# Transposing the norms' results on VectorE and by DMA instead of on TensorE, in a graph network and attention kernel

## The chip, the cores and the metric

The kernel runs on one core of a Trainium2 chip. The metric is the device time of that core in microseconds, from its first to its last instruction. Most executions of a kernel agree within 0.3%. A kernel under test and the kernel before it ran in turn on the same chip.

Engines in the profile: PE is TensorE (matrix products, and transposes as products with a unit matrix), DVE is VectorE, ACT is ScalarE, POOL is GpSimd, SP is the engine that issues most DMAs. PEclk is the share of the full clock that TensorE was granted.

## The reference, cut to what matters

```python
x   = graph_layer(x, adj, ...)     # 64 graphs, 256 nodes, 256 features, fp32
out = relational_attention(x, adj, ...)

def graph_layer(x, adj):
    h = gat(gat(x, adj, W1, a), adj, W2, a)
    h = layernorm(x + h) * g1 + b1                       # norm 0
    return layernorm(h + relu(h @ wf1 + bf1) @ wf2 + bf2) * g2 + b2    # norm 1

def relational_attention(x, adj):
    q, k, v_r = x @ Wq + bq, x @ Wk + bk, x @ Wv[r] + bv[r]
    p = softmax(q k^T / sqrt(32))                        # 8 heads
    a = sum over r of (p * (adj == r)) @ v_r
    x = layernorm(x + a @ Wo + bo) * g3 + b3             # norm 2
    return layernorm(x + gelu(x @ W1 + b1) @ W2 + b2) * g4 + b4        # norm 3
```

Only relations 0 and 1 occur, so the kernel keeps `v0` and `v1 - v0`. In these data all norm scales are 1 and all shifts and biases 0; the kernels do not rely on it unless it is said.

## The kernel before

Two graphs make a unit of 512 nodes, and 32 units go through a software pipeline. A turn handles attention and its feed-forward part of unit y, the first feed-forward part of unit y+1 and the graph attention of unit y+2. A norm's result lies with nodes on partitions; the product that follows needs features on partitions. So there are three transposed features in a turn: h1T (after norm 0, for the first feed-forward part), h2T (after norm 1, for q, k and v) and h3T (after norm 2, for the second feed-forward part).

```python
def to_features(src, name, scale=None, shift=None):
    dst = work.tile([P, KB, TN], F32, tag="hT", name=name)
    for k in range(KB):                                   # 2
        ps = bank(f"{name}p{k}")                          # one of 6 PSUM banks
        for t in range(T):                                # 4
            nc.tensor.transpose(ps[:, t * P:(t + 1) * P], src[:, t, k * P:(k + 1) * P], ident)
        ...                                               # VectorE: out of PSUM, * scale + shift

def normed(u, l, y, ...):
    ...                                                   # VectorE: bn_stats, mean, variance
    nc.vector.tensor_scalar(ve, variance, EPS, ...)       # 128x4
    nc.gpsimd.tensor_tensor(rs, ve, mhalf, ALU.pow)       # 128x4
    for t in blocks:                                      # VectorE: (y - mean) * rs, in place
        nc.vector.tensor_scalar(y[:, t, :], y[:, t, :], mv[:, t, 0:1], rs[:, t:t + 1], ...)

def affine(u, l, xn, g, b, r=None):                       # the norm's scale and shift: the residual
    ...                                                   # r: 128 x (4*256)
    nc.gpsimd.tensor_mul(r, xn, g[:, None, :].to_broadcast(list(r.shape)))
    nc.gpsimd.tensor_add(r, r, b[:, None, :].to_broadcast(list(r.shape)))

def weighted(u, b, m, q, k_, aT):                         # "scores": one graph, four heads
    ...                                                   # PE: 8 products into 4 banks (sp)
    for a in range(HPB):                                  # ScalarE: e = exp(sp)
        nc.scalar.activation(e[:, a, :], ps[a], AF.Exp, scale=isd)
    for a in range(0, HPB, 2):                            # VectorE: ea = e * mask, 128x1024 twice
        nc.vector.tensor_tensor(ea[:, a:a + 2, :], e[:, a:a + 2, :],
                                ab[:, None, :].to_broadcast([P, 2, NB * N]), ALU.mult)
    nc.vector.tensor_add(es, e[:, :, 0:N], e[:, :, N:2 * N])
```

The order of TensorE in a turn: h2T, the second graph sums (ygp), q, k, two blocks of v, h1T, two blocks of v, scores 0, hidden 0 to 2, scores 1, sums 0 (po, zo), and so on. Each block of v takes a PSUM bank until VectorE has added the bias and written it to SBUF. Only TensorE's order is fixed by hand; the other engines' orders come from a scheduler.

Of the kernel before, what the change touches and what calls it, by code (L numbers as in the profile page):

```python
# [16 lines left out]
P = 128  # L17
# [368 lines left out]
def narrow_path(  # L386
# [42 lines left out]
    def load(u):  # L429


        xs = io.tile([P, T, F], F32, tag="xs", name=f"xs{u}")
        nc.sync.dma_start(xs, x[G * u:G * (u + 1)].rearrange("b (c p) f -> p (b c) f", p=P))
        xq = io.tile([P, KB, TN], F32, tag="xq", name=f"xq{u}", bufs=1)
        aq = io.tile([P, T, N], I32, tag="aq", name=f"aq{u}", bufs=1)
        xu = x[G * u:G * (u + 1)].rearrange("b (n r) (k q c) -> q k r (b n) c", r=32, k=KB, c=32)
        au = adj[G * u:G * (u + 1)].rearrange("b (n r) (j q c) -> q b r j n c", r=32, j=NB, c=32)
        for q in range(Q):
            qp = slice(q * 32, (q + 1) * 32)
            for k in range(KB):  # L440
                nc.sync.dma_start(xq[qp, k, :].rearrange("r (n c) -> r n c", c=32), xu[q, k])
            for b in range(G):
                nc.sync.dma_start(aq[qp, b * NB:(b + 1) * NB, :].rearrange("r j (n c) -> r j n c", c=32),
                                  au[q, b])
        return xs, xq, aq
# [50 lines left out]
    def row(v, name):  # L496
        n = v.shape[0]
        t = const.tile([P, n], F32, name=name)
        nc.sync.dma_start(t, bass.AP(tensor=v.tensor, offset=v.offset, ap=[[0, P], [1, n]]))
        return t  # L500
# [42 lines left out]
    rbf2, rbo, rbt2 = row(g_bf2, "rbf2"), row(t_bo, "rbo"), row(t_b2, "rbt2")  # L543
# [13 lines left out]
    nc.gpsimd.tensor_add(rb1, rb1, rbf2)  # L557
    nc.gpsimd.tensor_add(rb2, rb2, rbo)
    nc.gpsimd.tensor_add(rb3, rb3, rbt2)


    def to_features(src, name, scale=None, shift=None):

        dst = work.tile([P, KB, TN], F32, tag="hT", name=name)
        for k in range(KB):
            ps = bank(f"{name}p{k}")
            for t in range(T):
                nc.tensor.transpose(ps[:, t * P:(t + 1) * P], src[:, t, k * P:(k + 1) * P], ident)
            if scale is None:
                nc.vector.tensor_copy(dst[:, k, :], ps)  # L570
            else:
                nc.vector.tensor_scalar(dst[:, k, :], ps, scale[:, k:k + 1], shift[:, k:k + 1],  # L572
                                        op0=ALU.mult, op1=ALU.add)
        return dst

    def adjacency(u, aq):
# [3 lines left out]
        return aT  # L580

# [18 lines left out]
    def projected(u, hT):  # L600
        xp = work.tile([P, T, WX], F32, tag="wh", name=f"xp{u}")
        for t in range(T):
            ps = bank(f"xpp{u}_{t}")
            for k in range(KB):
                nc.tensor.matmul(ps[:, :WX], hT[:, k, t * P:(t + 1) * P], gwe[:, k, :],  # L605
# [82 lines left out]
    def hidden(u, l, hT, wi, bi, func, blocks, h1=None):  # L688
# [3 lines left out]
        for f in blocks:  # L692
            ps = bank(f"h1p{u}_{l}_{f}")
            for k in range(KB):
                nc.tensor.matmul(ps, wi[:, k, f * P:(f + 1) * P], hT[:, k, :],  # L695
# [3 lines left out]

    def hidden_out(u, l, h1, wo_, res):  # L700
        y = work.tile([P, T, F], F32, tag="y", name=f"yf{u}_{l}")
        for b in range(G):
            add_blocks(u, f"yfp{l}_", y, res, b, lambda t, k: h1[:, k, t * P:(t + 1) * P],
                       lambda b, k: wo_[:, k, :], FB)
        return y

    def queries_keys(u, hT):
        qk = []
        for w, c, name in ((wq, bq, "q"), (wk, bk, "k")):
            d = work.tile([P, KB, TN], F32, tag=name, name=f"{name}{u}", bufs=1)  # L710
            for m in range(KB):
                ps = bank(f"{name}p{u}_{m}")
                for k in range(KB):
                    nc.tensor.matmul(ps, w[:, k, m * P:(m + 1) * P], hT[:, k, :],  # L714
# [5 lines left out]
    def values(u, hT, blocks, v=None):  # L720
# [3 lines left out]
        for t in blocks:  # L724
            ps = bank(f"vp{u}_{t}")
            for k in range(KB):
                nc.tensor.matmul(ps, hT[:, k, t * P:(t + 1) * P], wvf[:, k, :],  # L727
# [53 lines left out]
    def early(z):  # L781

        d = g[z]
        d["xT"] = work.tile([P, KB, TN], F32, tag="hT", name=f"xT{z}")
        nc.vector.transpose(d["xT"].rearrange("p k n -> p (k n)"), d["xq"].rearrange("p k n -> p (k n)"))
# [14 lines left out]
    def second_sums(x_):  # L800
# [8 lines left out]
        d["res"] = affine(x_, 0, d["y"], rg1, rb1)  # L809
# [3 lines left out]
    def out_pieces(u, h1, res):  # L813
# [3 lines left out]
        for b in range(G):  # L817
            ps = bank(f"yfp1_{u}_{b}")
            for i in range(NB):
                t = b * NB + i  # L820
                for k in range(FB):
                    nc.tensor.matmul(ps[:, i * F:(i + 1) * F], h1[:, k, t * P:(t + 1) * P], w2[:, k, :],  # L822
                                     start=(k == 0), stop=(k == FB - 1))
                if i == NB - 1:
                    bt = slice(b * NB, (b + 1) * NB)
                    nc.vector.tensor_tensor(y[:, bt, :].rearrange("p t f -> p (t f)"), ps,
                                            res[:, bt, :].rearrange("p t f -> p (t f)"), ALU.add)
                    normed(u, 3, y, range(b * NB, (b + 1) * NB))
                    affine(u, 3, y[:, bt, :], rg4, rb4, r[:, bt, :])
                    nc.sync.dma_start(out[G * u + b].rearrange("(c p) f -> p c f", p=P), r[:, bt, :])  # L830
                yield

    def piece(_=None):
# [3 lines left out]
    def turn(y_, x_, z):  # L837
        def have(u):
            return 0 <= u < NG

        if y_ == 0:
            g[z]["xs"], g[z]["xq"], g[z]["aq"] = load(z)
        if z + 1 < NG:
            g[z + 1]["xs"], g[z + 1]["xq"], g[z + 1]["aq"] = load(z + 1)
        Y, X, Z = g.get(y_, {}), g.get(x_, {}), g.get(z, {})
        if have(y_):
            hT = to_features(Y["y"], f"h2T{y_}", lg2, lb2)
        if have(x_) and y_ > 0:
            second_sums(x_)
        if have(y_):  # L850
            q, k_ = queries_keys(y_, hT)
            v = values(y_, hT, range(T // 2))
        if have(x_):
            h1hT = to_features(X["y"], f"h1T{x_}", lg1, lb1)
        if have(y_):
            values(y_, hT, range(T // 2, T), v)
            quads = [(b, m) for b in range(G) for m in range(KB)]
            aT = Y["aT"]
            oT = q
            acc = [None] * G  # L860
            e = {}

            def scores(n):
                e[n] = weighted(y_, *quads[n], q, k_, aT)

            def apply_(n):
                b, m = quads[n]
                if m == 0:
                    acc[b] = [psum.tile([P, 512], F32, tag=t_, name=f"{t_}{y_}_{b}") for t_ in ("po", "zo")]
                applied(b, m, v, *e.pop(n), *acc[b])  # L870
                if m == KB - 1:
                    divided(y_, b, *acc[b], oT)

        h1 = None

        def steps():
            if have(y_):
                yield scores, 0
            yield hid, range(0, 3)
            if have(y_):  # L880
                yield scores, 1
                yield piece, None
                yield apply_, 0
            yield hid, range(3, 4)
            if have(y_):
                yield scores, 2
                yield apply_, 1
            yield hid, range(4, 6)
            if have(y_):
                yield scores, 3  # L890
                yield piece, None
            yield hid, range(6, 8)
            if have(z):
                yield early, z
            if have(y_):
                yield apply_, 2
                yield apply_, 3

        def hid(blocks):
            nonlocal h1  # L900
            if have(x_):
                h1 = hidden(x_, 0, h1hT, wf1, bf1, AF.Relu, blocks, h1)

        for do, what in steps():
            do(what)
        if have(y_):
            yo = work.tile([P, T, F], F32, tag="y", name=f"yo{y_}")

            def out_(b):
                add_blocks(y_, "yop", yo, Y["res"], b, lambda t, k: oT[:, k, t * P:(t + 1) * P],  # L910
                           lambda b, k: wo[:, k, :], KB)
            out_(0)
            piece()
        if have(z):
            project(z)
        if have(y_):
            out_(1)
        if have(z):
            first_scores(z)
        if have(y_):  # L920
            yn = normed(y_, 2, yo)
            res = affine(y_, 2, yn, rg3, rb3)
            piece()
        if have(x_):
            yf = hidden_out(x_, 0, h1, wf2, X["res"])
            X["y"] = normed(x_, 1, yf)
            X["res"] = affine(x_, 1, X["y"], rg2, rb2)
        if have(y_):
            hT = to_features(yn, f"h3T{y_}", lg3, lb3)
        if have(z):  # L930
            Z["hp"] = gat_first(z, Z["s"], Z["xp"])
        if have(y_):
            h1 = hidden(y_, 1, hT, w1, b1, AF.Gelu, range(FB))
        if have(z):
            second_scores(z)
            checked(z, Z["aq"])
        if y_ == NG - 2:
            left.append(out_pieces(y_, h1, res))
        elif y_ == NG - 1:
            for _ in out_pieces(y_, h1, res):  # L940
                pass
        else:
            yf = hidden_out(y_, 1, h1, w2, res)
            yn = normed(y_, 3, yf)
            res = affine(y_, 3, yn, rg4, rb4)
            nc.sync.dma_start(out[G * y_:G * (y_ + 1)].rearrange("b (c p) f -> p (b c) f", p=P), res)
# [78 lines left out]
```

## Time and profile before

| | before |
|---|---|
| time, median of 6 runs | 3293.18 us (3292.28 to 3294.46) |
| TensorE busy | 3244.5 us, 99% of 3290.2 |
| VectorE, ScalarE, GpSimd busy | 56%, 32%, 29% |
| a turn | 100.6 us |
| the 24 transposes of a turn | 2.63 us |

The prediction shows how these are read. Two timelines of the kernel before, GpSimd's and VectorE's (start, duration, engine, line, operation, output and inputs with their shapes, count; in brackets the idle time before it and what ended it):

```profile
2017.82 2.37 POOL L684 TENSOR_TENSOR res<-yg,rg 128x1024 f32<-128x1024 f32 x1 [1.50 <-DVE yg L676]
2020.27 2.36 POOL L685 TENSOR_TENSOR res<-res,rb 128x1024 f32<-128x1024 f32 x1
```

```profile
2025.48 2.36 DVE L751 TENSOR_TENSOR ea<-e,aT 128x1024 f32<-128x1024 f32 x2 [0.33 <-ACT e L749]
```

The last residual ends at 2022.63, the first masking starts at 2025.48. Its two instructions take 2.36 us together, 1.18 us each.

### The profile page before, as it was taken

The numbers are of one execution on the slowest core, as the hardware profiler recorded it, in microseconds if no ns is written. First come the engines' busy times: TensorE is split into PE (matmuls) and PEld (weight loads), VectorE is DVE, ScalarE is ACT, GpSimd is POOL, SyncE is SP. The second block draws the span as 40 slices with busy tenths as digits, with TensorE's granted clock in tenths as the row PEclk, the third lists the DMA queues.
The fourth block names the chain that finished last, engine by engine and source line by source line (L and its number), as shares of the span: only waits on it lengthen the run. The fifth ranks groups of instructions, "written<-read, shape, count | busy, mean of one in ns | idle before, by whom it ended". The sixth has DMA issues, their size and how long they took to land.

```text
span 3290.2 us, 42867 instructions
## 1 busy us (share of the span) xinstructions
PE 3244.5 (99%) x17468; PEld 2105.4 (64%) x17468; DVE 1853.9 (56%) x3611; ACT 1050.6 (32%) x1860; POOL 960.7 (29%) x822
## 2 busy tenths in 40 slices
PE   7999999999999999999999999999999999999997
PEld 5656666666666566666666665666666666656655
DVE  3654556655556545566555565455665555654545
ACT  3233233332332332333323323323333233233221
POOL 2223323233232233232332322332323323223322
PEclk9999999999999999999999999999999999999999
DMA  5110001101011100011010111000110101110000
GB/s 140 20 25 21 20 14 27 26 20 24 9 26 27 25 22 20 14 26 27 20 24 10 26 27 25 21 20 14 27 27 20 24 10 26 26 24 10 7 1 14
DMA packets 294859, 76.65 MB, mean 23 GB/s; under 512 B 254936, under 2 KB 294016, under 8 KB 294656
## 3 DMA queue, kind: packets, MB, share of 16 engines
q1 hardware_dynamic: 293248, 72.52, 10.0%
q8 instruction: 139, 2.28, 0.3%
q0 software_dynamic: 1056, 1.05, 0.2%
q14 instruction: 64, 0.52, 0.1%
q10 hardware_dynamic: 352, 0.28, 0.0%
HBM read 57.04 MB, written 16.78 MB: 22 GB/s over the span
## 4 chain that ended last, share of the span: by engine, by line
PE 96%; DVE 1%; issue 1%; DMA 1%; POOL 0%; SPq 0%; ACT 0%; ACTq 0%; POOLq 0%; DVEq 0%
PE h1p L695 27%; PE yfp L654 26%; PE po L764 7%; PE vp L727 7%; PE sp L743 4%; PE yop L654 3%; PE qp L714 3%; PE hpp L643 3%; PE xpp L605 3%; PE kp L714 3%; PE ygp L654 3%; PE zo L767 2%; PE rows L615 1%; PE yfp L822 1%; DVE rz L772 0%
## 5 line engine op out<-in xcount | busy, mean ns | idle before, releaser
L697 ACT ACTIVATE h<-h1p,cols 128x512 f32<-128x512 f32 x512 | 353.0, 690 | 531.2 <-PE h1p L695 530.0
L695 PE MATMUL h1p<-h1T,wf 128*128 128x512 f32 x1024 | 474.3, 606 | 0.1
L654 PE MATMUL yfp<-wf,h 128*128 128x256 f32 x2048 | 447.3, 379 | 0.0
L695 PE MATMUL h1p<-h3T,w 128*128 128x512 f32 x1024 | 445.4, 593 | 1.8 <-DVE h3T L572 1.8
L654 PEld LDWEIGHTS yfp<-wf,h 128*128 128x128 f32 x2048 | 386.8, 190 | 51.8 <-issue 0.5
L654 PE MATMUL yfp<-w,h 128*128 128x256 f32 x1920 | 419.4, 379 | 0.0
L751 DVE TENSOR_TENSOR ea<-e,aT 128x1024 f32<-128x1024 f32 x256 | 320.2, 1291 | 162.9 <-ACT e L749 162.9
L654 PEld LDWEIGHTS yfp<-w,h 128*128 128x128 f32 x1920 | 362.5, 190 | 48.0
L773 POOL TENSOR_TENSOR low<-low,rz 128x512 f32<-128x512 f32 x64 | 82.4, 1288 | 1002.2 <-DVE rz L772 1002.2
L749 ACT ACTIVATE e<-sp 128x512 f32<-128x512 f32 x512 | 264.2, 604 | 301.3 <-PE sp L743 300.0
L695 PEld LDWEIGHTS h1p<-h3T,w 128*128 128x128 f32 x1024 | 194.2, 190 | 234.2 <-issue 228.6
L695 PEld LDWEIGHTS h1p<-h1T,wf 128*128 128x128 f32 x1024 | 184.8, 190 | 232.5 <-issue 178.0
L624 DVE SCALAR_TENSOR_TENSOR s<-s 128x512 f32<-128x512 f32 x128 | 87.1, 681 | 427.3 <-ACT s L621 426.1
L657 DVE TENSOR_TENSOR yf<-yfp,res 128x512 f32<-128x512 f32 x124 | 85.8, 692 | 395.4 <-PE yfp L654 393.4
L685 POOL TENSOR_TENSOR res<-res,rb 128x1024 f32<-128x1024 f32 (+1 forms) x130 | 301.1, 2316 | 10.2
L672 POOL TENSOR_TENSOR rs<-ve,mhalf 128x4 f32<-128x4 f32 (+1 forms) x130 | 131.0, 1008 | 414.1 <-DVE ve L671 413.9
L727 PE MATMUL vp<-wv,h2T 128*128 128x512 f32 x512 | 230.1, 592 | 0.0
L772 DVE RECIPROCAL rz<-zo 128x512 f32<-128x512 f32 x64 | 214.6, 3354 | 4.9 <-PE zo L767 2.5
L716 ACT ACTIVATE q<-qp,cols 128x512 f32<-128x512 f32 x64 | 44.0, 687 | 530.6 <-PE qp L714 530.6
L645 ACT COPY hp<-hpp 128x258 f32<-128x258 f32 x128 | 47.3, 375 | 423.6 <-PE hpp L643 423.6
L684 POOL TENSOR_TENSOR res<-yf,rg 128x1024 f32<-128x1024 f32 (+1 forms) x66 | 151.0, 2288 | 96.2 <-DVE yf L676 95.4
L727 PEld LDWEIGHTS vp<-wv,h2T 128*128 128x128 f32 x512 | 94.9, 190 | 107.6 <-issue 107.6
(408 smaller groups left out, 4210.4 us busy)
## 6 DMA issues: line engine op xcount, KB each, us to landing
xs<-in_x_dram SPq DMA_DIRECT2D x32, 512.0 KB, 3.7
xq<-in_x_dram SPq DMA_DIRECT2D x240, 64.0 KB, 2.2
aq<-in_adj_dram SPq DMA_DIRECT2D x240, 64.0 KB, 2.4
out_dram<-res SPq DMA_DIRECT2D x30, 512.0 KB
wf<-in_L_gnn_w_ff_dram SPq DMA_DIRECT2D x2, 1024.0 KB, 7.2
w<-in_L_gnn_W_dram SPq DMA_DIRECT2D x2, 1024.0 KB
first<-in_adj_dram POOLq DMA_DIRECT2D x2, 512.0 KB, 7.5
out_dram<-res SPq DMA_DIRECT2D x4, 256.0 KB, 2.1
```

Of the source, the lines that this page charges most:

```text
L654: nc.tensor.matmul(ps[:, i * F:(i + 1) * F], lhs(t, k), rhs(b, k), start=(k == 0), stop=(k == n - 1))
L684: nc.gpsimd.tensor_mul(r, xn, g[:, None, :].to_broadcast(list(r.shape)))
L685: nc.gpsimd.tensor_add(r, r, b[:, None, :].to_broadcast(list(r.shape)))
L695: nc.tensor.matmul(ps, wi[:, k, f * P:(f + 1) * P], hT[:, k, :], start=(k == 0), stop=(k == KB - 1))
L697: nc.scalar.activation(h1[:, f, :], ps, func, bias=bi[:, f:f + 1])
L714: nc.tensor.matmul(ps, w[:, k, m * P:(m + 1) * P], hT[:, k, :], start=(k == 0), stop=(k == KB - 1))
L727: nc.tensor.matmul(ps, hT[:, k, t * P:(t + 1) * P], wvf[:, k, :], start=(k == 0), stop=(k == KB - 1))
L743: nc.tensor.matmul(ps[a][:, j * N:(j + 1) * N], k_[hp, m, j0:j0 + P], q[hp, m, b * N:(b + 1) * N], start=True, stop=True)
L749: nc.scalar.activation(e[:, a, :], ps[a], AF.Exp, scale=isd)
L751: nc.vector.tensor_tensor(ea[:, a:a + 2, :], e[:, a:a + 2, :], ab[:, None, :].to_broadcast([P, 2, NB * N]), ALU.mult)
L764: nc.tensor.matmul(po[hp, m * N:(m + 1) * N], vs[:, hp], w[:, a, j * N:(j + 1) * N], start=(n == 0), stop=(n == len(terms) - 1))
L772: nc.vector.reciprocal(rz, zo)
```

## The change

The intent is to take the three transposes of a turn off TensorE, which bounds the kernel. VectorE transposes 32x32 blocks, each within its own 32 partitions, and 16 DMAs carry the blocks to their partitions. As no eviction is left that could apply a norm's scale and shift, these are folded into the next weights and biases at the start. To give the DMAs time, ygp moves to the end of the turn before, and the first scores go ahead of v. The order of SP is now fixed by hand too.

```diff
+    def normed_features(u, l, xn, natural=False):
+        yt = work.tile([P, Q, KB, T, 32], F32, tag="yt", name=f"yt{u}_{l}", bufs=1)
+        for t in range(T):
+            nc.vector.transpose(yt[:, :, :, t].rearrange("p q k r -> p k q r"),
+                                xn[:, t].rearrange("p (k q c) -> p k q c", k=KB, c=32))
+        ...                                  # h2T (natural): the same with runs of 128 bytes
+        hT = work.tile([P, Q, KB, T, 32], F32, tag="hT", name=f"hT{u}_{l}")
+        for q in range(Q):
+            for a in range(Q):
+                nc.sync.dma_start(hT[q * 32:(q + 1) * 32, a], yt[a * 32:(a + 1) * 32, q])
+        return [hT[:, :, k].rearrange("p a t r -> p t a r") for k in range(KB)]
...
+    shifted(wf1, FB, lb1, bf1, "bf1")        # bias += weights^T shift, on TensorE; also wq, wk, w1, wv
+    for w, scale in ((wf1, lg1), (wq, lg2), (wk, lg2), (wv..., lg2), (w1, lg3)):
+        for k in range(KB):
+            nc.gpsimd.tensor_scalar(w[:, k], w[:, k], scale[:, k:k + 1], 1.0, ...)
...
     def turn(y_, x_, z):
-        hT = to_features(Y["y"], f"h2T{y_}", lg2, lb2)
-        second_sums(x_)
         q, k_ = queries_keys(y_, hT)
-        v = values(y_, hT, range(T // 2))
-        h1hT = to_features(X["y"], f"h1T{x_}", lg1, lb1)
-        values(y_, hT, range(T // 2, T), v)
-        scores 0; hidden 0-2; scores 1; sums 0; hidden 3; scores 2; sums 1; hidden 4-5; scores 3; ...
+        scores(0)
+        v = values(y_, hT, range(T))
+        scores(1); sums(0); hidden 0-1; scores(2); sums(1); hidden 2-4; scores(3); hidden 5-7; ...
...
-        hT = to_features(yn, f"h3T{y_}", lg3, lb3)
+        hT = normed_features(y_, 2, yn)
...
+        for t in range(T):
+            if t == T - 1:
+                second_sums(z)               # ygp and norm 0, one turn earlier
+            hidden_out_block(y_, 1, yf, h1, w2, res, t)
+        first_residual(z)                    # GpSimd: affine of norm 0
+        yn = normed(y_, 3, yf)
+        res = affine(y_, 3, yn, rg4, rb4)    # GpSimd: affine of norm 3
```

(The lines of the turn are abridged.)

## The prediction

> **What bounds the kernel now.** 64 graphs go through in 32 units of two; a software-pipelined turn handles three units at once (attention and feed-forward of unit y, first feed-forward of y+1, graph attention of y+2). I read the page's busy row and its chain first, to see which engine sets the end.
>
> ```profile
> PE 3244.5 (99%) x17468; PEld 2105.4 (64%) x17468; DVE 1853.9 (56%) x3611; ACT 1050.6 (32%) x1860; POOL 960.7 (29%) x822
> ...
> PE 96%; DVE 1%; issue 1%; DMA 1%; POOL 0%; SPq 0%; ACT 0%; ACTq 0%; POOLq 0%; DVEq 0%
> ```
>
> TensorE is the path; nothing else reaches 60%. A removed matmul is therefore worth its full pitch, and an added wait of TensorE costs its full length. Then TensorE in order of time over one turn in the middle (start, duration, group; durations overlap in the pipeline, so I use differences of starts):
>
> ```profile
> 2023.20 1.15 PE L743 MATMUL sp<-q,k 32*128 32x256 f32 x16
> ...
> 2072.39 1.04 PE L568 MATMUL h3T19p<-ident,yo 128*128 128x128 f32 x8
> 2073.27 3.65 PE L643 MATMUL hpp<-xp,s 128*128 128x258 f32 x16
> ...
> 2104.74 1.04 PE L568 MATMUL h2T20p<-ident,yf 128*128 128x128 f32 x8
> 2105.61 3.62 PE L654 MATMUL ygp<-hp,s 128*128 128x256 f32 x16
> ...
> 2119.36 1.04 PE L568 MATMUL h1T21p<-ident,yg 128*128 128x128 f32 x8
> 2120.24 3.60 PE L727 MATMUL vp<-wv,h2T 128*128 128x512 f32 x8
> ...
> 2123.77 1.15 PE L743 MATMUL sp<-q,k 32*128 32x256 f32 x16
> ```
>
> No line carries a wait. A turn is 2123.77 - 2023.20 = 100.57 us, and 30 like it follow from 112.5. The three groups of eight transposes hold TensorE for 0.88, 0.87 and 0.88 us: 2.63 us a turn. That is all that the change can take out of a turn. Last the start, where TensorE does wait (brackets: idle before):
>
> ```profile
> 14.34 1.18 PE L590 MATMUL aTp<-ident,first 128*128 128x128 f32 x8
> ...
> 22.88 1.04 PE L568 MATMUL xT1p<-ident,xs 128*128 128x128 f32 x8
> 32.00 5.26 PE L605 MATMUL xpp<-gwe,xT 128*128 128x260 f32 x16 [8.08 <-DVE xT L570]
> ...
> 96.02 5.40 PE L714 MATMUL qp<-h2T,wq 128*128 128x512 f32 x8 [2.05 <-DVE h2T L572]
> ```
>
> **What the Trainium skill says.** "VectorE: DVE Perf Modes", section "The three transpose paths": VectorE transposes 32x32 blocks only, TensorE a whole 128x128 into PSUM. So the blocks must still be moved between partitions, here by 16 DMAs each. The trace has the form: the transpose of 128x1024 fp32 (xT) takes 1.24 us, which I read as some 0.3 to 0.4 us for 128x256. "DMA: Bandwidth & Descriptors", section "Anatomy of one DMA", puts the fixed cost of a DMA at about 2 us, mostly the receipt of the write. The trace agrees: 64 KB pieces land 2.2 us (xq) and 2.4 us (aq) after their issue. "TensorE: Matmul & The Clock Gate", section "What's actually happening": after an idle window of about 3.4 us the array runs at half clock until warm. The trace agrees: the 16 xpp instructions after 8.08 us idle took 5.26 us, in the middle of the run 3.67 us.
>
> **What is removed.** Of 96 transposed features (3 for each of 32 units) three stay on TensorE (h1T of unit 0, h2T of unit 0, h3T of unit 31). 93 x 0.877 = 81.6 us leave TensorE's path. VectorE loses 186 evictions with scale and shift of 0.79 us, some 140 us, and gets 93 x 4 = 372 transposes of 128x256, about as much. Off the path, so neutral.
>
> **What is added in a turn.** Per feature: four VectorE transposes (about 1.5 us), 16 DMAs of 32 KB from one queue, and the landing. The issue is the long part. In the before trace eight xq issues took 4.05 us and cost 0.31 to 0.49 us each; small two-dimensional ones cost 0.24 to 0.28:
>
> ```profile
> 2025.18 4.05 SPq L441 DMA_DIRECT2D xq<-in_x_dram  x8
> ```
>
> I take 0.33 us for h1T and h3T (32 runs of 1 KB) and 0.45 for h2T (runs of 128 B): 16 x 0.33 = 5.3 us or 7.2 us, plus 2 us. With 1.5 us in front the added latency is about 9 us, or 11. Does TensorE reach the consumer earlier? Counting with pitches of the trace (0.429 us for a 512-wide instruction, 0.216 for 256):
>
> h3T: the norm's last pass ends at 2065.6 here.
>
> ```profile
> 2063.80 1.83 DVE L676 TENSOR_SCALAR yo<-yo,mv,rs 128x256 f32<-128x256 f32 x4 [1.00 <-POOL rs L672]
> ```
>
> Transposed by 2067.1, issued by 2072.5, landed by 2074.5. It is wanted after yfp and hpp, 2076.75 - 0.88 = 2075.9. Slack 1.3 us: the tightest.
> h1T: made near the end of the turn before, about 3 us after q's start in the new order; landed at 10.5; wanted after q, k, scores, v, scores and the first sums, at 18.2. Slack near 8 us.
> h2T: yf is normed 5 us after its matmuls, lands some 18 us after them, wanted 35 us after them.
> The new order also leaves 8 us instead of 6.4 between a unit's first scores and their sums. VectorE has v's four evictions in there and is some 9 us in arrears from the two norms, but by my count is ready by 15.6 for 15.9. Buffers: hT has two, and in the new order each is read before it is refilled. So a turn should be 100.57 - 2.63 = 97.9 us, with a chance of a small wait at h3T.
>
> **What is added once, at the start.** The folding of shifts is 40 matmuls of one column (80 instructions) and two of 512. The order of instructions puts all of them on TensorE ahead of aTp, and the last 16 need w1, one of the last weights to come. Before, aTp began at 14.34. The queue moves 300 to 370 GB/s; the bytes up to w1 are 7.9 MB, passed at about 27 us, landed at 28 to 29. The 16 matmuls are 32 instructions at 0.11 us warm or 0.22 cold (gwap in the trace has 0.22), some 5 us; rbv's four take 1.7. So aTp begins near 35. From aTp to the second xpp it is VectorE and ScalarE, some 13.7 us by the durations of the trace (transposes 2, copies with the check 2.5, xpp 3.9, rows 0.9, the softmax's first passes with the second check 4.4); the old run had 17.7, 8 of it waiting, since VectorE stood behind wv:
>
> ```profile
> 27.27 0.69 DVE L551 TENSOR_TENSOR wv<-wv 128x512 f32<-128x512 f32 x1 [9.28 <-DMA wv<-in_L_gnn_Wv_dram]
> ```
>
> The new xpp comes at 48.7 instead of 32.0: about 17 us late (14 to 19). The scaling of weights on GpSimd (some 11 us) ends before its first softmax work.
> A second loss is before turn 0. VectorE's order has h2T0's copies behind the whole norm of unit 1 and its four transposes. Before they ran ahead of it:
>
> ```profile
> 95.18 0.79 DVE L572 TENSOR_SCALAR h2T<-h2T0p,cols 128x512 f32<-128x512 f32 x1
> ...
> 99.16 1.38 DVE L676 TENSOR_SCALAR yg<-yg,mv,rs 128x256 f32<-128x256 f32 x4 [1.13 <-POOL rs L672]
> ```
>
> The norm ends at 100.5 (it waits for GpSimd's residual), transposes 102.0, first copy 102.65: q starts 6.6 us later.
>
> **At the end.** In turn 30 q follows directly on 13.7 us of hidden matmuls; h2T of unit 31 needs about 15.5: a wait of 2 us for 0.56 before. Two waits for h3T (0.9) go, and v between the first scores of turn 31 should save 2 us of the waits there. Sum -1.5.
>
> **Sum.** 3293.4 - 81.6 + 17 + 6.6 - 1.5 = 3233.9. For a chance of about one third that h3T or a bank waits, 0 to 1 us in 30 turns, I add 2: 3236, 1.7% faster.
>
> **Rivals.** (1) The start costs little, because the weights come earlier or the loss is caught up: nothing on TensorE in the start waits for data after qp, so what is lost there stays lost; but with w1 at 26 and a warm clock the loss is 20 instead of 24, and 3230. With no loss at all it would be 3212, 2.5% faster. (2) The DMAs come too late for h3T every turn: if an issue takes 0.45 us instead of 0.33, 1.9 us more, so 0.6 us a turn, about 18 us, and 3252; at 0.6 us an issue it is 3 us a turn and the change is worth nothing (3325). For it: aq's issues with four dimensions do take 0.63; against: this transfer has two dimensions, and the 128-row loads with 1 KB rows take 0.43. (3) VectorE becomes the bound in the first third of a turn, where its arrears hold back a PSUM bank and so k or the scores: 0.8 us of slack at k's second bank; a slower strided transpose, or a wait for a port while GpSimd works, would make it 0.5 us a turn, 15 us, 3250. (4) Moving operands in 128-byte runs are read more slowly: no such case is in the trace; half of the 512-wide matmuls of hidden would be hit. I think it unlikely.
>
> **Range and chances.** The gain in the turns is nearly certain in size, 81 us; the losses range from 20 to 60. That gives 3216 to 3262. The 2% line is 3227.5, 8 us under my number, and only a smaller loss in the start gets there: 0.22. Slower by 2% needs over 4 us of waiting a turn: 0.03.
>
> **What would show it.** Right: a turn of 97.9 us with no wait of TensorE; aTp near 35; a wait of about 9 us before the first qp; hT issues near 0.33 us. Wrong: h1p waiting for hT's DMA in each turn, a turn over 98.5, aTp before 30, or hidden's instructions off their 0.429 us pitch.

## The result and the profile after

The changed kernel takes 3512.59 us (median of 6 runs, 3506.42 to 3528.74) against 3293.18 us. The ratio is 1.0672, with a 95% interval of 1.0651 to 1.0692. Ratios here are the mean time of one kernel's fast runs over that of the other's of the same rounds, so not quite the ratio of the medians. The prediction was 3236 us with a range up to 3262. It was wrong.

The page's busy row and its chain of waits, after:

```profile
PE 3345.5 (95%) x16808; PEld 2103.9 (60%) x16808; DVE 1991.0 (56%) x3802; ACT 1054.2 (30%) x1860; POOL 994.2 (28%) x832
...
PE 71%; DVE 15%; SPq 8%; DMA 2%; POOL 2%; issue 1%; ACT 1%; DVEq 0%; ACTq 0%; POOLq 0%
```

TensorE was 96% of the chain; now VectorE holds 15% of it and the issuing of DMAs 8%. TensorE is busy for 101.0 us more with 660 fewer instructions. 81.6 us of transposes are gone, so what is left takes 182.6 us longer. Most of this is slow clock: the mean granted clock was 0.961 over 3527.0 us, against 0.996 over 3290.2 us before, which makes about 138 us of lost clock against 13 (one minus the clock, times the span). The folding's instructions at the start are some 20 us of the rest, and waits too short to be listed are in it too. Idle time rose from 45.7 to 181.5 us, 135.8 more. The two together, less the 81.6, are the 236.8 us between the spans of the two profiles, 3527.0 and 3290.2. (The profiled execution is the longest of the six, 3528.7 us, 16 us above the median.)

The view of TensorE's waits (what waited, for what: total us, times, longest):

```profile
PE h1p L737 <- DMA hT<-yt: 78.8, 30, 3.5
PE sp L799 <- DVE v L785: 52.7, 30, 1.9
```

Two waits that come once in nearly every turn are new: hidden (h1p) waits for h3T's DMAs, and the second scores (sp) wait for VectorE to clear a bank of v. TensorE in order of time over a turn:

```profile
2022.82 13.97 PE L737 MATMUL h1p<-hT,w 128*128 128x512 f32 x32 [2.33 <-DMA hT<-yt]
...
2061.30 1.15 PE L799 MATMUL sp<-q,k 32*128 32x256 f32 x16
...
2071.88 1.72 PE L799 MATMUL sp<-q,k 32*128 32x256 f32 x12 [1.74 <-DVE v L785]
2073.53 1.86 PE L820 MATMUL po<-e,v 128*32 128x256 f32 x16
...
2129.19 16.05 PE L737 MATMUL h1p<-hT,w 128*128 128x512 f32 x30 [3.48 <-DMA hT<-yt]
```

The three lines of eight transposes are gone, as intended. The wait of 1.74 us is followed by slow instructions: the 16 po products take 1.86 us here and 1.07 us at the next sums. The hidden after 3.48 us takes over 16 us; after 2.33 us it takes its full-clock 13.97. The mean turn is 107.5 us where 97.9 was predicted.

**The first wait** starts at the queue. SP's timeline, the 16 copies of the h3T that made TensorE wait 3.48 us:

```profile
2116.70 10.90 SPq L621 DMA_DIRECT2D hT<-yt  x16
```

This is 0.68 us an issue, and the slowest of the 31 h3T: most take 10.0 us, 0.63 us an issue. A copy lands 1.9 us after its own issue begins (median). Over all turns, TensorE comes to hidden 9.1 us after h3T's last block transpose, and the copies are complete 11.7 us after it; the difference is the mean wait of 2.6 us.

**The second wait** starts on GpSimd. GpSimd's and VectorE's timelines in the same turn:

```profile
2055.96 2.35 POOL L726 TENSOR_TENSOR res<-yg,rg 128x1024 f32<-128x1024 f32 x1 [1.50 <-DVE yg L718]
2058.39 2.35 POOL L727 TENSOR_TENSOR res<-res,rb 128x1024 f32<-128x1024 f32 x1
...
2063.36 2.36 POOL L726 TENSOR_TENSOR res<-yf,rg 128x1024 f32<-128x1024 f32 x1 [1.50 <-DVE yf L718]
2065.80 3.21 POOL L727 TENSOR_TENSOR res<-res,rb 128x1024 f32<-128x1024 f32 x1
```

```profile
2058.82 1.94 DVE L713 TENSOR_SCALAR ve<-mv 128x4 f32<-128x4 f32 x1
...
2063.58 6.51 DVE L807 TENSOR_TENSOR ea<-e,aT 128x1024 f32<-128x1024 f32 x2 [0.29 <-ACT e L805]
...
2071.15 2.47 DVE L785 TENSOR_TENSOR v<-vp,rbv 128x512 f32<-128x512 f32 x4
```

The residuals of norms 0 and 3 now lie on top of norm 3's passes and the first masking. A 128x4 instruction takes 1.94 us (0.17 where GpSimd is idle) and ends when the GpSimd instruction does. The two ea take 6.51 us instead of 2.36. That is what comes out if the first runs when `res<-yf,rg` has ended, at 2065.72, and the second when `res<-res,rb` has ended, at 2069.01: with its 1.18 us the second would end at 2070.19, and the two do end at 2070.09. GpSimd's 3.21 us instead of 2.35 are the other side of it. V's evictions stand behind them on VectorE. That VectorE and GpSimd can exclude each other for whole instructions is what the Trainium skill says in "SBUF — State Buffer", section "SBUF: two separate sides": they share a pair of ports, held as an exclusive lock for the whole instruction, by a VectorE instruction in a two-port mode or with two SBUF inputs (the latter only against a GpSimd instruction that reads SBUF), or by GpSimd's. The trace agrees, to a tenth of a microsecond.

**The start** went as predicted within a few microseconds (aTp: transposes of the first adjacency; xpp: the graph layer's first products; the last line is the first q):

```profile
36.67 1.91 PE L632 MATMUL aTp<-ident,first 128*128 128x128 f32 x8
...
50.22 6.81 PE L647 MATMUL xpp<-gwe,xT 128*128 128x260 f32 x16 [2.95 <-DVE xT L594]
...
122.91 6.25 PE L770 MATMUL qp<-h2T,wq 128*128 128x512 f32 x8 [8.38 <-DVE h2T L594]
```

The first q starts 26.9 us later than before (96.02).

### The profile page after: what moved, and what is told of

Read it like the earlier page. It is cut to its first block, busy times and chain, and to the rows that moved or that the text cites. A ratio compares the mean times of both kernels' runs of the same rounds, so it can differ in the third digit from the quotient of the medians.

```text
span 3527.0 us, 43810 instructions
## 1 busy us (share of the span) xinstructions
PE 3345.5 (95%) x16808; PEld 2103.9 (60%) x16808; DVE 1991.0 (56%) x3802; ACT 1054.2 (30%) x1860; POOL 994.2 (28%) x832
## 4 chain that ended last, share of the span: by engine, by line
PE 71%; DVE 15%; SPq 8%; DMA 2%; POOL 2%; issue 1%; ACT 1%; DVEq 0%; ACTq 0%; POOLq 0%
PE h1p L737 27%; PE yfp L748 13%; PE po L820 8%; SPq L621 7%; DVE ea L807 6%; PE sp L799 5%; PE xpp L647 3%; PE yop L696 3%; PE qp L770 3%; PE kp L770 3%; PE ygp L696 3%; PE zo L823 2%; DMA hT<-yt 2%; DVE yo L718 1%; DVE s L669 1%
## 5 line engine op out<-in xcount | busy, mean ns | idle before, releaser
L807 DVE TENSOR_TENSOR ea<-e,aT 128x1024 f32<-128x1024 f32 x256 | 424.7, 1699 | 265.1 <-ACT e L805 264.0
L737 PE MATMUL h1p<-hT,w 128*128 128x512 f32 x992 | 476.7, 642 | 81.4 <-DMA hT<-yt 78.8
L748 PE MATMUL yfp<-w,h 128*128 128x256 f32 x2048 | 452.9, 379 | 0.0
L737 PE MATMUL h1p<-hT,wf 128*128 128x512 f32 x992 | 451.5, 603 | 0.0
L748 PEld LDWEIGHTS yfp<-wf,h 128*128 128x128 f32 x2048 | 387.9, 191 | 52.3 <-issue 0.5
L748 PEld LDWEIGHTS yfp<-w,h 128*128 128x128 f32 x2048 | 386.6, 190 | 52.3 <-issue 0.8
L737 PEld LDWEIGHTS h1p<-hT,w 128*128 128x128 f32 x992 | 202.0, 207 | 343.0 <-issue 337.6
L727 POOL TENSOR_TENSOR res<-res,rb 128x1024 f32<-128x1024 f32 (+1 forms) x130 | 326.8, 2514 | 10.2
L737 PEld LDWEIGHTS h1p<-hT,wf 128*128 128x128 f32 x992 | 181.8, 191 | 233.5 <-issue 186.4
L799 PE MATMUL sp<-q,k 32*128 32x256 f32 x2048 | 201.5, 426 | 52.7 <-DVE v L785 52.7
L799 PEld LDWEIGHTS sp<-q,k 32*128 32x128 f32 x2048 | 116.6, 192 | 175.3 <-issue 96.0
L783 PE MATMUL vp<-wv,hT 128*128 128x512 f32 x496 | 221.1, 599 | 0.0
```

The source lines that it names most:

```text
L737: nc.tensor.matmul(ps, wi[:, k, f * P:(f + 1) * P], hT[k], start=(k == 0), stop=(k == KB - 1))
L748: nc.tensor.matmul(ps[:, i * F:(i + 1) * F], h1[:, k, t * P:(t + 1) * P], wo_[:, k, :], start=(k == 0), stop=(k == FB - 1))
L783: nc.tensor.matmul(ps, hT[k][:, t * P:(t + 1) * P], wvf[:, k, :], start=(k == 0), stop=(k == KB - 1))
L799: nc.tensor.matmul(ps[a][:, j * N:(j + 1) * N], k_[hp, m, j0:j0 + P], q[hp, m, b * N:(b + 1) * N], start=True, stop=True)
```

## The experiments

The theory: the change loses (A) about 2.6 us a turn and some slow clock because one queue takes 10 to 11 us to issue 16 copies, and (B) about as much because GpSimd's residuals hold the masking up, and it behind v. The rival to B: VectorE is simply in arrears with its own new work, and the long ea is a side effect. Thirteen kernels were run, all with correct results. The times of the kernel before in their rounds lie between 3292.4 and 3294.0 us (medians).

| run | what it is | us | ratio to before |
|---|---|---|---|
| after | the change | 3512.6 | 1.067 |
| e1 | h3T back on TensorE | 3416.5 | 1.037 |
| e2 | another form of the masking | 3514.1 | 1.067 |
| e3 | h3T's copies from two queues | 3383.5 | 1.027 |
| e4 | e2 and e3 | 3380.6 | 1.026 |
| b1 | before, with the new order | 3385.3 | 1.028 |
| b2 | the same, h1T left in place | 3450.0 | 1.048 |
| c1 | e3 without GpSimd's residuals 0 and 3 | 3241.8 | 0.984 |
| d1 | e3, masking queued behind v | 3384.7 | 1.028 |
| d2 | e3, residuals later | 3343.0 | 1.015 |
| f1 | e3, residuals in short instructions | 3276.2 | 0.995 |
| f4 | the change, residuals in short instructions | 3379.5 | 1.027 |
| f2 | f1 with another start | 3255.8 | 0.989 |
| g1 | f2, residuals later and short, last h2T on TensorE | 3210.6 | 0.975 |

### e1 and e3: the queue

e1 puts h3T back on TensorE in every turn:

```diff
-        if X:
-            hT = normed_features(y_, 2, yn)
...
+        hT = to_features(yn, f"h3T{y_}")
```

e3 keeps the change and lets ScalarE's queue issue half of h3T's copies:

```diff
-                nc.sync.dma_start(hT[q * 32:(q + 1) * 32, a], yt[a * 32:(a + 1) * 32, q])
+                queue = nc.scalar if l == 2 and a % 2 else nc.sync
+                queue.dma_start(hT[q * 32:(q + 1) * 32, a], yt[a * 32:(a + 1) * 32, q])
```

> The changed kernel with h3T alone back on TensorE in all units. Theory A (the 16 issues for h3T, 0.65 us each, come too late: 2.6 us wait per turn, and hidden's first matmuls then run at half clock, some 1.6 us more): the wait of h1p for hT goes, hidden is back at 13.7 us, 0.9 us of transposes return, so 3.4 us less a turn, about 3410 us. Rival (the wait only hides another that ends at the same place, or the slow clock comes from the DMA traffic and not from the wait): the time stays within 30 us of 3512.

> The changed kernel with half of h3T's 16 issues on ScalarE's queue, which is idle there. Theory A: the issue takes 5.3 us instead of 10.9, hT lands 1 us or more before it is wanted, the wait of h1p and its slow start go: 4.2 us less a turn, about 3385 us. Rival (the transfers or their landing, not the issue, take the time): the wait stays above 2 us and the time near 3512.

Both came in as expected: 3416.5 and 3383.5 us. In both, hidden's wait is gone and the wait of sp for v stays at 52.4 and 52.3 us. With two queues, SP issues its eight in 5.28 us, 0.66 us each: an issue is no cheaper, but two go on side by side. The queue cost 129 us (3512.6 - 3383.5), of which 79 are the waits themselves; the rest, some 50 us, fits the slow clock after them: e3's mean granted clock is 0.977 over 3383.7 us, about 78 us of lost clock, 60 less than in the profile of the change. So part A stands.

### e2 and e4: a form of the masking that GpSimd might not hold up

```diff
-            nc.vector.tensor_tensor(ea[:, a:a + 2, :], e[:, a:a + 2, :],
-                                    ab[:, None, :].to_broadcast([P, 2, NB * N]), ALU.mult)
+            nc.vector.scalar_tensor_tensor(ea[:, a:a + 2, :], e[:, a:a + 2, :], 1.0,
+                                           ab[:, None, :].to_broadcast([P, 2, NB * N]),
+                                           op0=ALU.mult, op1=ALU.mult)
```

> The changed kernel with ea = e * adjacency as a scalar_tensor_tensor instead of a tensor_tensor, all else the same. Theory B (tensor_tensor of two SBUF operands is locked out while GpSimd runs a residual; ea's two instructions of the first scores take 6.5 us instead of 2.4, so v is evicted late and the second scores wait 1.8 us and then run at half clock, some 3 us): if scalar_tensor_tensor does not take part in the lock, the two take 2.4 us again, the wait of sp for v goes, 4 to 5 us less a turn, about 3370 us. Rival (VectorE is simply in arrears from two norms and the transposes, or any VectorE instruction is held up there): ea stays near 6 us in total and the time at 3512.

> e2 and e3 together. Theory A and B: both waits and both slow stretches go, a turn is near the 97.9 us that the removal of the transposes alone gives, and the time near 3235 to 3245 us with the start still 25 us longer than before. Rival (a third wait stands behind the two): a turn over 100 us, over 3300 us.

Both missed. All ea together take 424.8 us in e2, 424.7 in the change: this form is held up in just the same way. It also reads two tensors from SBUF, and by the section cited above that is what counts. e4 is as slow as its rival, "a third wait", had it, but shows none: TensorE still waits 52.6 us for v. The runs say nothing for or against B, only that the remedy was none.

### c1: the residuals taken away

On e3. With scale 1 and shift and bias 0 the residual is the norm's result itself, so GpSimd's four instructions for norms 0 and 3 can be left out (this is right on these data alone). The result tiles then live longer and get a third buffer, the residuals give one up.

```diff
-        g[x_]["res"] = affine(x_, 0, g[x_]["y"], rg1, rb1)
+        g[x_]["res"] = g[x_]["y"]
...
-        yn = normed(y_, 3, yf)
-        res = affine(y_, 3, yn, rg4, rb4)
+        res = normed(y_, 3, yf)
```

> The changed kernel with two issuing queues for h3T, and GpSimd's scale and shift of norms 0 and 3 left out (four 128x1024 instructions a turn; right on these data alone, where scales are 1 and shifts 0). Theory B, in which these instructions hold VectorE's masking up: the first two ea instructions take 2.4 us instead of 6.5, no wait for v, a turn near 98 us, 3235 to 3255 us. Rival, in which VectorE is in arrears by its own work: the wait for v stays within 0.5 us of its 1.75, a turn of 102 to 103 us, 3360 to 3385 us.

3241.8 us, inside what B expects, and 142 us below e3. VectorE's timeline in c1:

```profile
1993.82 2.36 DVE L808 TENSOR_TENSOR ea<-e,aT 128x1024 f32<-128x1024 f32 x2 [2.15 <-ACT e L806]
...
1999.79 0.69 DVE L786 TENSOR_TENSOR v<-vp,rbv 128x512 f32<-128x512 f32 x1 [0.67 <-PE vp L784]
```

The masking is back at 2.36 us. VectorE waits at both lines, for ScalarE's exponentials and for TensorE's product, and TensorE no longer waits for VectorE. A turn is 97.93 us, the predicted 97.9 to the tenth. This settles B against its rival: VectorE's own new work leaves it ahead of TensorE. The moved buffer is no way out: d2 and f1 below leave the buffers as they are, and there too the wait for v is gone. Of the 142 us, 52 are the waits and about 45 slow clock (0.990 over 3240.0 us is about 32 us of lost clock, e3 has 78); the rest is not listed as a wait.

### b1 and b2: the new order alone

Both are the kernel before, transposes on TensorE and nothing folded, with scores 0 ahead of v and the hidden blocks in their new places. b1 also moved h1T ahead of all of v; b2, whose edit is shown, left it between the halves of v.

```diff
             q, k_ = queries_keys(y_, hT)
+            scores(0)
             v = values(y_, hT, range(T // 2))
         if have(x_):
             h1hT = to_features(X["y"], f"h1T{x_}", lg1, lb1)
         ...
-            yield hid, range(0, 3)        # and 3-4, 4-6, 6-8
+            ...                           # hid 0-2, 2-5, 5-8, each behind scores or sums
```

> The kernel before with only the new order of its turn (first scores ahead of all values, hidden blocks in the new places); transposes stay on TensorE, nothing is folded. Theory B, in which the wait of the scores for v comes of the new order (the first scores' masking is put between VectorE's queue and v's evictions while GpSimd writes residuals): TensorE waits 1.5 to 2 us for v in each turn, a turn of 102 to 105 us, 3350 to 3430 us. Rival, in which the wait comes of VectorE's and the queue's new work (block transposes, results one turn earlier): no such wait, a turn of 100.6 us, 3285 to 3300 us.

> As b1, but the transposes of h1T keep their old place between the two halves of v (b1 had moved them ahead of v, and its wait was theirs). If the new order alone brings VectorE's masking between GpSimd's residuals and v's evictions: TensorE waits for v or for h1T in each turn, a turn over 101.5 us, 3320 to 3400 us. Rival, in which the wait needs the block transposes and the norm that the change puts on VectorE one turn earlier: a turn within 0.5 us of 100.6, 3285 to 3310 us.

b1 took 3385.3 us, inside the interval expected under B, but for another reason: TensorE waited for norm 0 (1.39 us in one turn) before the transposes that this edit had moved up. It does not count for B. b2 took 3450.0 us, more than expected, and shows the wait that was looked for. TensorE's waits, then VectorE's and GpSimd's timelines, in b2:

```profile
PE sp L743 <- DVE v L729: 48.0, 29, 1.7
```

```profile
1368.36 4.52 DVE L751 TENSOR_TENSOR ea<-e,aT 128x1024 f32<-128x1024 f32 x2
1372.80 3.37 DVE L754 TENSOR_TENSOR es<-e 128x1024 f32<-128x1024 f32 x1
1376.09 1.27 DVE L729 TENSOR_TENSOR v<-vp,rbv 128x512 f32<-128x512 f32 x2
```

```profile
1368.43 3.36 POOL L684 TENSOR_TENSOR res<-yg,rg 128x1024 f32<-128x1024 f32 x1 [1.50 <-DVE yg L676]
1371.87 3.21 POOL L685 TENSOR_TENSOR res<-res,rb 128x1024 f32<-128x1024 f32 x1
```

The mean turn is 105.8 us instead of 100.6. So the new order is enough to bring the collision about: with scores 0 ahead of v, the masking moves up into the residuals by the 8 us that v and h1T take on TensorE, and v's evictions are behind it. In the old order v was evicted first, and the residuals were over when the masking began.

### d1: masking given to the scheduler behind v

On e3, the two ea of scores 0 are emitted behind the four blocks of v.

```diff
-        v = values(y_, hT, range(T))
+        v = values(y_, hT, range(T))
+        mask(0)                            # the ea of scores 0, no longer in scores(0)
```

> The changed kernel with two issuing queues for h3T, and the masking of the first scores given to the scheduler behind v's evictions (in the order on VectorE only one of v's evictions, and not the others, moves ahead of es). Theory B: the two held up ea instructions still stand ahead of v, the wait for v shrinks by little, 3370 to 3385 us. If it was es that v waited for: the wait falls by 1 us, 3320 to 3350 us.

3384.7 us, at the upper end of what B expects: the two ea still stand ahead of v on VectorE, since the scheduler finds their inputs ready sooner. Only one eviction of v moved ahead of es. The wait for v is 50.1 us in 59 pieces instead of 52.3 in 30. It was not es that v waited for.

### d2 and f1: the residuals later, or in short instructions

d2 (on e3) fixes GpSimd's order by hand too, and writes both residuals behind the third sums, where GpSimd first waits for the division of the first half (norm 2 also moves ahead of the graph scores in the program). f1 (on e3) leaves them where they are and cuts each of GpSimd's 128x1024 instructions into four of 128x256:

```diff
-        nc.gpsimd.tensor_mul(r, xn, g[:, None, :].to_broadcast(list(r.shape)))
-        nc.gpsimd.tensor_add(r, r, b[:, None, :].to_broadcast(list(r.shape)))
+        for t in range(r.shape[1]):
+            nc.gpsimd.tensor_mul(r[:, t, :], xn[:, t, :], g)
+            nc.gpsimd.tensor_add(r[:, t, :], r[:, t, :], b)
```

> The changed kernel with two issuing queues for h3T, and GpSimd's residuals of norms 0 and 3 written later in the turn, behind the third sums, by fixing GpSimd's order too. Theory B: the first two ea instructions take 2.4 us, no wait for v, a turn near 98 us unless the residuals collide with something there that TensorE waits for: 3240 to 3270 us. Rival (VectorE's own arrears): wait for v stays at 1.5 us or more, 3350 to 3385 us.

> The changed kernel with two issuing queues for h3T, and each GpSimd scale and each shift of a residual written as four instructions of 128x256 instead of one of 128x1024; nothing is left out, results hold for any data. If VectorE's masking is held for as long as GpSimd's instruction lasts (2.4 us), short instructions hold it for 0.6 to 0.7 us at a time: first two ea instructions near 3.5 us instead of 6.5, no wait for v, a turn of 98 us, 3240 to 3260 us. Rival: what counts is GpSimd's total time in the stretch, so that short instructions follow each other and ea is held as long as before: 3370 to 3400 us.

d2 took 3343.0 us: better by 40, but 73 above the upper end expected. There is no wait for v; the collision has moved to the last masking of the turn, where TensorE now waits 38.8 us for es and 53.2 us for the divided result. d2's VectorE:

```profile
1373.77 3.38 DVE L808 TENSOR_TENSOR ea<-e,aT 128x1024 f32<-128x1024 f32 x1
1377.08 3.40 DVE L811 TENSOR_TENSOR es<-e 128x1024 f32<-128x1024 f32 x1
```

One ea instead of 1.18 us takes 3.38, the es instead of 1.22 us 3.40: each waits out a whole residual instruction. d2 also shows a wait that costs its length alone: TensorE waits twice in each turn, 1.29 us for es and then, in the same turn,

```profile
2098.24 1.97 PE L697 MATMUL yop<-wo,q 128*128 128x256 f32 x8 [1.74 <-DVE q L831]
```

for the result, and the granted clock was 1.00 over the whole turn. The 92 us of waits cost 101 us against c1 (3343.0 - 3241.8).

f1 took 3276.2 us, 107 better than e3 and 16 above the range. Its VectorE timeline:

```profile
2015.62 3.41 DVE L809 TENSOR_TENSOR ea<-e,aT 128x1024 f32<-128x1024 f32 x2
```

The two ea take 3.41 us, the 3.5 that was expected, since each waits for a piece of some 0.7 us only. No wait of a microsecond is left, but the second scores take 2.28 us instead of 1.15, by the look of it for want of banks, and the mean turn is 99.07 us; these 1.1 us are the whole distance to c1's turn of 97.93. The expectation left out that norm 3's passes and es are held up too (four passes in 2.27 us, 1.38 without GpSimd; es in 1.74 us, not 1.22). Length counts, and so does place.

### f4: do the two waits add up?

f4 is the change with f1's short instructions and a single queue.

> The changed kernel with the short GpSimd instructions alone; h3T's 16 copies still come from one queue. If the two waits add up, this leaves the wait for hT's DMA (2.6 us a turn and slow instructions after it): 3514 - 142 = 3372 us, 3355 to 3390. If one wait hides the other, over 3400 us or under 3340.

3379.5 us, as expected from the sum. The short instructions gain 133 us with one queue and 107 with two (3383.5 - 3276.2), so the two losses add up only roughly: with short residuals the one queue costs 103 us (3379.5 - 3276.2), not 129.

### f2: the start

On f1: the folding stands in TensorE's waits of the start instead of ahead of everything, the difference of the value weights goes from VectorE to GpSimd, and h2T of unit 0 is copied ahead of unit 1's norm.

```diff
-    shifted(wf1, ...); shifted(wq, ...); shifted(wk, ...); shifted(w1, ...); rbv; scaling of all weights
...
         early_first(1)
+        fold_first()                       # wf1, while VectorE works on unit 0
         ...
+        second_matmuls(0); g[0]["y"] = normed(0, 0, ...)
+        fold_attention()                   # wq, wk, wv, while norm 0 is made
         ...
-        second_sums(1)
+        second_matmuls(1)
         g[0]["hT"] = to_features(yf, "h2T0")
+        second_norm(1)
+        fold_last()                        # w1
```

> f1_short_residuals with another start: the folding of shifts stands in TensorE's waits of the start instead of ahead of everything, the difference of value weights is on GpSimd, and VectorE copies h2T0 ahead of unit 1's norm. Expected, if the prediction's account of the start is right (24 us lost there, of which all but 3 to 8 can be had back): aTp near 14.5 us, first qp at 96 to 104 us instead of 121 to 123, 17 to 26 us less than f1 of the same rounds, 3215 to 3235 us. Rival (what is lost in the start is caught up elsewhere, or the folding still stalls TensorE because the weights come late): less than 8 us below f1.

f2 is 20.4 us faster than f1 (3255.8), as the account of the start expects, though 21 above the absolute range, which was set before f1 was known. TensorE in f2's start:

```profile
14.94 1.97 PE L642 MATMUL aTp<-ident,first 128*128 128x128 f32 x8
...
100.77 5.96 PE L781 MATMUL qp<-h2T,wq 128*128 128x512 f32 x8
```

aTp is back at its place of before and the first q starts 22 us earlier than in the change. What the start lost was not caught up anywhere.

### g1: everything

g1 is f2 with GpSimd's order fixed and the residuals both late (as in d2) and short (as in f1), so that they fall behind the first half's division, and with the last unit's h2T transposed by TensorE, where the DMAs made TensorE wait (4.0 us in e3 and c1, 4.9 in f2).

```diff
         sums(2)
+        while owed:
+            owed.pop(0)()                  # affine of norm 3, out, affine of norm 0 (short)
         sums(3)
...
-            X["hT"] = normed_features(x_, 1, X["y"], natural=True)
+            X["hT"] = normed_features(...) if z < NG else to_features(X["y"], f"h2T{x_}")
...
+    with tc.manual_schedule(engines={PE, SP, Pool}):
```

> f2_start with GpSimd's order fixed too: the two residuals are written behind the first half's division, in short instructions, where the next masking has several microseconds to spare (d2 had them there in long instructions and waited 1.3 and 1.7 us a turn); and the last h2T is transposed by TensorE. If where and in how long pieces GpSimd works is all that was wrong: a turn of 98 us, no waits in turns, 3210 to 3232 us. Rival (GpSimd's total work keeps costing TensorE something wherever it stands): a turn of 98.7 or more, 3240 to 3275 us.

3210.6 us (3209.6 to 3215.8), ratio 0.9749 with an interval of 0.9736 to 0.9763. It beats both kernels: 2.5% faster than the one before, with results right for any data. No wait of TensorE in a turn is listed any more, and the turn is 97.93 us. GpSimd's residuals still cost VectorE something, but where there is time. VectorE in g1:

```profile
2071.01 2.36 DVE L820 TENSOR_TENSOR ea<-e,aT 128x1024 f32<-128x1024 f32 x2 [2.08 <-ACT e L818]
...
2094.93 2.89 DVE L820 TENSOR_TENSOR ea<-e,aT 128x1024 f32<-128x1024 f32 x2 [1.23 <-ACT e L818]
2097.74 1.75 DVE L823 TENSOR_TENSOR es<-e 128x1024 f32<-128x1024 f32 x1
```

The first masking is free of GpSimd. The last one lies on the short residuals (2.89 us and es 1.75 us), and ends at 2099.49, before its sums want it. GpSimd is busier than in any other of these kernels (1211.7 us, 38%, because short instructions cost more in total), and that costs nothing.

## Why the prediction was wrong, point by point

- **What is removed** (81.6 us): right. In c1 and g1, where nothing else is in the way, a turn is 97.93 us, and 97.9 was predicted.
- **The cost of an issue** ("I take 0.33 us for h1T and h3T"): wrong, and the first step that failed. From one issue to the next it took 0.63 us for h3T and 0.64 for h1T on average, and 0.66 for h2T instead of 0.45 (the issue alone 0.59 and 0.61, medians). The number was taken from copies between DRAM and SBUF in the kernel before; no copy from SBUF to SBUF was in its trace. And it is near the lowest of those: the line that the prediction shows, eight in 4.05 us, is 0.51 us an issue (median of all 0.49). The page had a better warning, the adjacency's issues at 0.63 us, which the prediction named and set aside. The parts beside it were right: four block transposes in 1.42 us (about 1.5), landing 1.9 us after the issue (2).
- **Slack of h3T, 1.3 us**: with the right issue this becomes the wait of rival 2, which said "3 us a turn" at 0.6 us an issue. Measured: 2.6 us on average. The rival's mechanism was right and the size of the wait too. Its chance was too low (the prediction gave a wait at h3T or for a bank one chance in three, and at most 1 us), and its cost: 90 us in the rival, 129 measured.
- **VectorE "by my count is ready by 15.6 for 15.9"**: wrong, and the larger loss (142 us, against 129 for the queue). The count used durations from a trace in which GpSimd was quiet at that time. Rival 3 named "a wait for a port while GpSimd works" and gave it 0.5 us a turn. With the slow clock and the smaller waits that came with it, it was 4.7 us (142 / 30). The reordering moved the masking onto the residuals: b2 shows that the order alone does it, c1 that the residuals are the cause. What was missing in the working is a look at where GpSimd's four long instructions would lie after the change.
- **The clock after a wait**: left out. The prediction cited the rule of the slow clock for the start and charged each wait in the turns with its length alone. Here the 79 us of waits for the queue cost 129, and the 52 us of waits for v cost 142. The granted clock was below full in the 5 us after all 30 waits for v, and after 23 of the 30 waits for h3T. But it is no fixed surcharge: it was below full after 11 of 30 such waits in f4, and after none of 60 in d2. So "an added wait of TensorE costs its full length" is the least that it costs.
- **The start** (17 + 6.6 us): right in mechanism, measured 26.9 us for 23.6 (w1's 32 instructions took 7.0 us, not 5, rbv's four 3.8, not 1.7). aTp at 36.67 (near 35), second xpp at 50.22 (48.7), a wait of 8.4 us before q (about 9). f2 won 20.4 us of it back.
- **The end**: predicted a wait of 2 us before the last unit's q; it was 1.6 in the change and 4.0 in c1, where the turns are shorter.
- **The range**: 3216 to 3262 does not come out of the prediction's own figures. A gain of 81.6 and losses of 20 to 60 give 3232 to 3272.
- **Rival 4** (strided moving operands are read more slowly): did not happen. The 512-wide hidden products that read 128-byte runs take 603 ns on average after and 606 before, and 12 of them 5.42 us in both.

The parts add up: 3293.2 - 81.6 + 26.9 for the start + 129 for the queue + 142 for the collision = 3509.5, against 3512.6 measured. As 129 and 142 are themselves differences of runs, what this tests is c1, the change without its two failed steps: 3238.5 by the sum, 3241.8 measured. Three things stay open. Why an issue between two places of SBUF takes 0.63 us was not looked into. Why the clock went down after some waits and not after others of the same length is not known. And the part of the 142 us that is neither a listed wait nor lost clock, some 45 us, was not separated by a run.

## What to carry to other kernels

When a change moves work in time, look at what the engine that is not in the diff will be doing then: here GpSimd's instructions, unchanged, cost more than anything that was added. Where VectorE and GpSimd must overlap, keep GpSimd's instructions short and put them where VectorE's results are not wanted soon; moving alone and shortening alone each won only part of it. Charge many small DMAs to the queue that issues them, with a duration of the same kind of copy, and take the length of a new wait of TensorE as its least cost: here it cost between 1.1 times (d2) and 2.7 times (e3 against c1) as much.

## What the Trainium skill lacked or had wrong

- "DMA: Bandwidth & Descriptors", "Issuing engines are not separate DMA queues", says that several issuing engines only save the time of issuing, usually small beside the DMA itself. Here it was the large part: 16 issues took 10.0 to 10.9 us, the landing 1.9 us, and a second queue saved 129 us of 3512.6. The section "Anatomy of one DMA", which is about DMAs issued by GpSimd (the prediction cites it for SP's), gives about 50 ns for the dispatch. The nearest to a cost of issuing is "a few hundred ns" on top of that, in "SBUF — State Buffer", section "The DMA setup-cost knee"; a figure for SP and a copy of 32 KB between SBUF places (0.63 to 0.66 us from one issue to the next) stands on no page.
- "TensorE: Matmul & The Clock Gate" puts the idle window at about 3.4 us, free-running. (Its section "A second HAM failure mode: psum-queue depth-cycling" lets the clock swing after frequent short idles too, without a length.) In the change a wait of 1.74 us was followed by the slow clock; in d2 one of 1.74 us was not. The windows view of the changed kernel (stretch, length, busy time and count of each engine, granted clock, share of the DMA engines, GB/s), before and after the 1.74 us:

```profile
2055.00:2071.80 16.80, 15.14 (x51) 6.45 (x49) 15.30 (x22) 4.81 (x8) 11.39 (x6) 1.00 0.23 67
2071.88:2077.52 5.64, 5.64 (x53) 2.87 (x53) 5.64 (x7) 2.06 (x4) 0.00 (x0) 0.70 0.46 114
```

  The granted clock is 1.00 and then 0.70. With two waits in each turn, all of them 3.5 us or less, the change lost about 138 us of clock; d2, also with two waits in each turn (1.3 and 1.8 us on average), lost about 30 (0.991 over 3340.4 us), as c1 without waits did.
- "SBUF — State Buffer" was right about the lock (ea 6.51 us instead of 2.36), and the prediction would have been better for applying it to the new order. It advises to schedule the work off the critical path; it does not say that short GpSimd instructions shorten the other's wait (ea 3.41 us with pieces of 128x256). Its list of VectorE instructions does not name block transposes, though its rule for instructions with one SBUF input covers them. They were not held up: 1.41 us for four while GpSimd worked on residuals in f1, 1.42 without.
